# A two-layer sparse graph network on one Trainium2 core: a fourth buffer of queries, paid for with the room of the first products

## The chip, the cores and the metric

The kernel runs on one core of a Trainium2 chip (trn2). The metric is the device time of one execution in microseconds. Before the change the median of three runs was 2462.93 us (2452.32 to 2464.49). The profile comes from one more execution, of 2575.64 us, with the profiler on; its times are used for shares and for single operations, not as the metric.

## The reference

Eight graphs share one adjacency matrix of 2048 nodes (symmetric, with self loops, about one edge in 256), and each node has 256 features. All data are fp32.

- Layer 0 is attention with 4 heads of 64 features over the neighbours of a node. Scores are q.k / 8, clipped to [-10, 10]; where there is no edge, the score is -10. The softmax runs over each chunk of 256 keys by itself, and the results of the 8 chunks are added. Then come Wo, the bias, a residual, a layer norm with gamma and beta, once more + x, and a layer norm without weights.
- Layer 1 is graph attention: Wh = h W, logits leaky_relu(s_src[i] + s_dst[j]) on the edges, softmax over all neighbours, the weighted sum of Wh, elu, the residual and a layer norm.

```python
scores = clip(einsum('bhnd,bhjcd->bhnjc', q, kc) / 8, -10, 10); scores = where(mask == 0, -10, scores)
ctx = einsum('bhnjc,bhjcd->bhnd', softmax(scores, axis=-1), vc)
x = layernorm(x + (layernorm(ctx @ Wo.T + bo + x) * gamma + beta))
```

## The kernel before

The adjacency is so sparse that the kernel never forms a dense score matrix. It first builds, for each node, the list of its neighbours (`edge_lists`), sorts the nodes by their number of neighbours, and cuts them into 16 tiles of 128 nodes. A tile has as many slots as its busiest node has neighbours: `CAPS = (24, 14, 13, 12, 11, 11, 10, 10, 9, 9, 8, 8, 7, 7, 6, 5)`. (A node without an edge in a chunk is handled by constants, and a dense path for denser inputs is compiled in and not taken here.)

Batches are handled two at a time: there are 4 groups `g` of `G = 2` graphs, and 16 tiles `t` in each, so layer 0 has 64 steps. Layer 1 takes four graphs at a time: two passes of 16 tiles, of which the first is woven between the layer-0 steps of groups 2 and 3.

**Tables.** For each group, `tables(g, t)` turns 128 nodes of x into keys, values and queries on TensorE and writes them to DRAM: keys and values to `kv_d` (L369), queries to the first half of a row of `qx_d` (L380). Two tiles make a chunk of 256 nodes: `load_x` (L314) loads a chunk of x into an `xt` buffer, of which there are two, and `chunk_x` (L322) transposes it (L334) at even t. The second half of a `qx_d` row holds x + beta, which the end of layer 0 needs: at odd t GpSimd adds beta to the chunk in place (L352), and it is stored (L353). The tables of group 0 are made while the edge lists are built; those of group g + 1 during the steps of group g. Group 3's steps make none.

**Gathers.** `fetch0` (L504) gathers, for each slot of a tile, the keys and values of one neighbour per node, by an indirect DMA that GpSimd issues (L469). Two slots make a unit, and the units lie in a ring of `RING = 14` buffers, which layer 1 shares. A last one fetches the nodes' own queries and x + beta into a `qx` buffer (L507), of which there are three. A unit's buffer is free when its weighted values have been summed on TensorE (`summed`, L494). A `qx` buffer is free when `finish0` has made the layer norm with x + beta (L625), a step after the tile's scores.

**Scores.** `scores0` (L511) multiplies a unit's gathered keys by the queries on VectorE and sums the products over the features in one of two ways. For two thirds of the units (`npe = len(units) - len(units) // 3`, the first ones) VectorE writes the products (L530) and TensorE transposes and sums them in PSUM (L541, with ScalarE's copy L547 and the product with a selection matrix L551). For the last `len(units) // 3` units VectorE multiplies in place (L555) and sums with a reduction (L557). Products for TensorE go into room that is not used any more: those of unit i into the keys of unit i - 1. The first unit has none before it and uses a buffer of its own, `prod`. A tile with an odd number of slots has one slot in its last unit.

**Softmax, context, end.** `softmax0` clips the scores (L571) and normalizes them; `context0` weights the values on VectorE (L481) and ScalarE (L487) and sums them on TensorE (L494); `finish0` is Wo, the residual and the norms (L613 to L628), and `rows1` makes the table of layer 1. In step k the program writes, in this order: the gathers of step k + 1, the scores of step k, softmax and context of a layer-1 tile where there is one, `rows1` of i - 2, `finish0` of i - 1, the tables of the next group, softmax and context of step k.

That order is not the one on the engines. When the program is built, a planner of the framework orders each engine's instructions by the order of the program, but lets later ones go ahead where it reckons that an earlier one isn't ready. Each engine then follows its list strictly: in the trace a small VectorE operation of layer 1 (L665) stands at 212.21 us, before the first product of layer 0 at 263.00 us. So where an instruction stands in the program gives its rank, and the planner decides on its place.

Of the kernel before, what the change touches and what calls it, by code (L numbers as in the profile page):

```python
# [9 lines left out]
F32 = mybir.dt.float32  # L10
# [4 lines left out]
ALU = mybir.AluOpType  # L15
AX = mybir.AxisListType

P = 128
H = 4
D = 64  # L20
DP = 8
NJ = D // DP
# [14 lines left out]
G = 2  # L37
UNIT = 2
# [133 lines left out]
def sparse_path(ctx: ExitStack, tc: tile.TileContext, keep, x, adj, Wq, bq, Wk, bk, Wv, bv, Wo, bo, gamma, beta, W, a,  # L172
                out):
    nc = tc.nc
    B, N, F = x.shape
# [146 lines left out]
    def chunk_x(g, t):  # L322
# [18 lines left out]
        xTs[g, t] = xT, xC, xt  # L341
        return xT

    def tables(g, t):
        if t % 2 == 0:
            chunk_x(g, t)
        xT, xC, xt = xTs[g, t - t % 2]
        rows = slice(t % 2 * P, (t % 2 + 1) * P)
        if t % 2:

            xv = xt.rearrange("p k (b f) -> p (k b) f", b=G)
            nc.gpsimd.tensor_tensor(xv, xv, beta_r.unsqueeze(1).to_broadcast([P, 2 * G, F]), op=ALU.add)  # L352
            nc.sync.dma_start(qx_d[g][(t - 1) * P:(t + 1) * P, GF:].rearrange("(k p) f -> p k f", p=P), xt)  # L353
        kvs = work.tile([P, 2 * GF + 1], F32, tag="kvs", name="kvs", bufs=1)
        if g == PG:
            nc.scalar.copy(kvs[:, 2 * GF:], rank[:, t:t + 1])
        vk = kvs[:, 0:GF].rearrange("p (j b f) -> p b j f", b=G, j=NJ)
        for b in range(G):
            pm = bank("tk")
            for kc in range(KC):  # L360
                nc.tensor.matmul(pm[:, 0:F], xT[:, b * KC + kc, rows], wkv[:, kc, 0:F], start=(kc == 0), stop=False,  # L361
                                 skip_group_check=True)
            add_bias(pm[:, 0:F], biasT[:, 1])
            for kc in range(KC):
                nc.tensor.matmul(pm[:, F:], xC[:, b * KC + kc, rows], wkv[:, kc, F:], start=False, stop=(kc == KC - 1),  # L365
                                 skip_group_check=True)
            nc.scalar.copy(vk[:, b], pm[:, 0:F].rearrange("p (j f) -> p j f", j=NJ))
            nc.scalar.copy(kvs[:, GF + b * F:GF + (b + 1) * F], pm[:, F:])  # L368
        nc.sync.dma_start(kv_d[g][t * P:(t + 1) * P, :], kvs[:, 0:kv_d[g].shape[1]])  # L369
        q = bank("tk")  # L370
        for b in range(G):
            qb = q[:, b * F:(b + 1) * F]
            for kc in range(KC):
                nc.tensor.matmul(qb, xT[:, b * KC + kc, rows], wq[:, kc, :], start=(b == 0 and kc == 0), stop=False,  # L374
                                 skip_group_check=True)
            add_bias(qb, biasT[:, 0])
        qs = work.tile([P, GF], F32, tag="qs", name="qs", bufs=1)
        nc.scalar.copy(qs.rearrange("p (j b f) -> p b j f", b=G, j=NJ),
                       q.rearrange("p (b j f) -> p b j f", b=G, j=NJ))
        nc.sync.dma_start(qx_d[g][t * P:(t + 1) * P, 0:GF], qs)  # L380
        if t == NT - 1:

            tot = small.tile([P, G, KC], F32, tag="tot", name="tot", bufs=1)
            nc.vector.tensor_reduce(tot, xsum.pop(g), axis=AX.X, op=ALU.add)
            mv = small.tile([P, KC, G], F32, tag="mvs", name="mvs", bufs=1)
            pv = bank("tk")[:, 0:KC * G].rearrange("p (c b) -> p c b", c=KC)
            for oc in range(KC):
                for kc in range(KC):
                    nc.tensor.matmul(pv[:, oc, :], wkv[:, kc, F + oc * P:F + (oc + 1) * P], tot[:, :, kc],
                                     start=(oc == 0 and kc == 0), stop=(kc == KC - 1), skip_group_check=True)  # L390
            for oc in range(KC):
                nc.scalar.activation(mv[:, oc, :], pv[:, oc, :], AF.Identity, scale=-1.0, bias=bvc[:, oc:oc + 1])
            bO = small.tile([P, G, KC], F32, tag="bO", name="bO")
            po = bank("tk")[:, 0:KC * G].rearrange("p (c b) -> p c b", c=KC)
            for oc in range(KC):
                for kc in range(KC):
                    nc.tensor.matmul(po[:, oc, :], wo[:, kc, oc * P:(oc + 1) * P], mv[:, kc, :],
                                     start=(oc == 0 and kc == 0), stop=(kc == KC - 1), skip_group_check=True)
            for oc in range(KC):
                nc.scalar.activation(bO[:, :, oc], po[:, oc, :], AF.Identity, bias=biasT[:, 2, oc:oc + 1])  # L400
            biasO[g] = bO

    def first_tables(t):
        if t == 0:
            load_x(0, 0)
        if t % 2 == 0 and t + 2 < NT:
            load_x(0, t + 2)
        tables(0, t)

    with tc.tile_pool(name="lists", bufs=1) as pool:  # L410
# [92 lines left out]

    def fetch0(g, t):  # L504
        units = gather(kv_d[g].shape[1], kv_d[g], idx, t)
        qx = work.tile([P, 2 * GF], F32, tag="qx", name="qx", bufs=3)
        nc.gpsimd.indirect_dma_start(out=qx, out_offset=None, in_=qx_d[g],  # L507
                                     in_offset=bass.IndirectOffsetOnAxis(ap=node[:, t:t + 1], axis=0))
        got0[g, t] = qx, units

    def scores0(g, t):  # L511
# [2 lines left out]
        q = qx[:, 0:GF]  # L514
        sc = small.tile([P, GH, S], F32, tag="sc", name="sc")

        npe = len(units) - len(units) // 3
        ps_sc = bank("tf")[:, 0:GH * S].rearrange("p (s e) -> p s e", e=GH)
        W8 = GH * DP
        qv = q.rearrange("p (k j w) -> p k j w", k=UNIT, w=W8).unsqueeze(3)  # L520
# [1 line left out]
        def product(i):  # L522

            u, s0, n = units[i]
            if i:
                room = units[i - 1][0][:, :, 0:GF]
            else:
                room = work.tile([P, UNIT, GF], F32, tag="prod", name="prod", bufs=1)
            prod = room.rearrange("p k (j w) -> p k j w", w=UNIT * W8)[:, :, :, 0:n * W8]
            nc.vector.tensor_tensor(prod.rearrange("p k j (s w) -> p k j s w", w=W8),  # L530
                                    u[:, :, 0:GF].rearrange("p s (k j w) -> p k j s w", k=UNIT, w=W8),
                                    qv.to_broadcast([P, UNIT, NJ // UNIT, n, W8]), op=ALU.mult)
            return prod

        for i in range(0, npe, 4):
            some = units[i:min(i + 4, npe)]
            pr = bank("pr", 1).rearrange("p (k r) -> p k r", r=P)
            for k, (u, s0, n) in enumerate(some):
                prod = product(i + k)
                for j in range(NJ):  # L540
                    nc.tensor.matmul(pr[0:n * W8, k, :], prod[:, j // (NJ // UNIT), j % (NJ // UNIT), :], ident, is_transpose=True,  # L541
                                     start=(j == 0), stop=(j == NJ - 1), skip_group_check=True)
            m = len(some)
            prT = work.tile([P, 4, P], F32, tag="prT", name="prT", bufs=1)
            full = m - 1 if some[-1][2] < UNIT else m
            if full:
                nc.scalar.copy(prT[:, 0:full, :], pr[:, 0:full, :])  # L547
            if full < m:
                nc.scalar.copy(prT[0:W8, full, :], pr[0:W8, full, :])
            for k, (u, s0, n) in enumerate(some):  # L550
                nc.tensor.matmul(ps_sc[:, s0:s0 + n, :], prT[0:n * W8, k, :], sel[0:n * W8, 0:n * GH],  # L551
                                 start=(s0 == 0), stop=(k == m - 1 and i + m == npe), skip_group_check=True)
        for u, s0, n in units[npe:]:
            prod = u[:, :, 0:GF].rearrange("p s (j w) -> p s j w", w=W8)
            nc.vector.tensor_tensor(prod, prod, q.rearrange("p (j w) -> p j w", w=W8).unsqueeze(1)  # L555
                                    .to_broadcast([P, n, NJ, W8]), op=ALU.mult)
            nc.vector.tensor_reduce(sc[:, :, s0:s0 + n].rearrange("p e s -> p s e"),  # L557
                                    prod.rearrange("p s j (e d) -> p s e j d", d=DP),
                                    axis=AX.XY, op=ALU.add)
        st0[g, t] = ps_sc, sc, min(S, UNIT * npe)  # L560


# [3 lines left out]
    def softmax0(g, t):  # L566
        S = CAPS[t]
        n = GH * S
        ps_sc, sc, sp = st0.pop((g, t))
        for some, dots in ((sc[:, :, 0:sp], ps_sc[:, 0:sp, :].rearrange("p s e -> p e s")), (sc[:, :, sp:], sc[:, :, sp:])):  # L570
            nc.vector.tensor_scalar(some, dots, -10.0, 10.0, op0=ALU.max, op1=ALU.min)  # L571
        e = ebuf[:, 0:n]
        ev = e.rearrange("p (e s) -> p e s", s=S)
        nc.scalar.activation(ev, sc, AF.Exp)
# [198 lines left out]
            (fetch1 if layer else fetch0)(*at(i))  # L773
            fetched[0] += 1

    load_x(1, 0)
    fetch(0)
    waiting = None
    for k, (layer, i) in enumerate(seq):
# [6 lines left out]
        if layer == 0:  # L786
# [11 lines left out]
            if i:  # L798
                finish0(*at(i - 1))
            if g + 1 < NG:  # L800
                if i % 2 == 0 and i + NT + 2 < NG * NT:
                    load_x((i + NT + 2) // NT, (i + 2) % NT)
                tables(g + 1, i % NT)
            if tables_first:
                fetch(k + 1)
# [449 lines left out]
```

## Time and profile before

| | |
|---|---|
| median of 3 runs | 2462.93 us (2452.32 to 2464.49) |
| profiled execution | span 2573.9 us, 38911 instructions |
| TensorE matmul / weight load | 75% / 64% |
| VectorE | 71% |
| ScalarE | 55% |
| GpSimd | 58% |
| DMA | 669.10 MB; gathers and scatters of GpSimd 505.01 MB |
| granted TensorE clock | 0.864 |

A line of the groups reads: line of the kernel, engine, operation, what is written <- what is read, shapes, count | busy us, mean ns of one | idle time of the engine just before these instructions, and what ended most of it. A line of the waits reads: engine, tile and line that waited <- what ended the wait: us in total, times, the longest. A line of a timeline reads: start in us, us, engine, line, operation, shapes, count [idle time before <- what ended it]. PE is TensorE, DVE is VectorE, ACT is ScalarE, POOL is GpSimd and SP is SyncE; L507 is line 507 of the kernel. `acc`, `tk`, `tf`, `mf` and `pr` are banks of PSUM.

The stages as the trace shows them: up to some 209 us the edge lists and the tables of group 0; from 255.64 us, where the first unit is gathered, to about 2100 us layer 0, with layer 1 woven in from about 1225 us; after that layer 1 alone.

### The profile page before, as it was taken

What the parts mean: (1) busy time and instruction counts of PE and PEld (TensorE: products, weight loads), DVE (VectorE), ACT (ScalarE), POOL (GpSimd) and SP (SyncE); (2) the same over time, 40 slices, a digit from 0 to 9 for tenths busy, and PEclk for the clock granted to TensorE, in tenths of its full rate; (3) what the DMA queues carried; (4) which work ended last, traced back from release to release, by engine and by line L of the source; (5) the groups of instructions that cost most, each with busy time, mean ns of one, the idle gap of its engine ahead of it and who ended that gap; (6) DMA issues with size and microseconds to landing.
All of it is one profiled execution on the core that took longest, in us unless ns stands there. A gap on an engine that the chain in (4) does not pass through costs nothing. (4 is left out here: it accounts for less than half of the span.)

```text
span 2573.9 us, 38911 instructions
## 1 busy us (share of the span) xinstructions
PE 1940.6 (75%) x11946; PEld 1657.1 (64%) x11946; DVE 1833.1 (71%) x4071; ACT 1408.0 (55%) x5011; POOL 1505.4 (58%) x1225
## 2 busy tenths in 40 slices
PE   6787787688878879989888877775856786555764
PEld 5675676577666767777777765664756675444654
DVE  5865567767557777767878797776877877656765
ACT  3573353355545455555555665654454567556756
POOL 1123655475545655655677667566757753667764
PEclk9888897898899999899999988886977887777877
DMA  6744977497877868887769878867769874986763
GB/s 217 261 154 159 330 254 256 149 336 254 292 259 243 279 221 307 294 299 271 264 239 369 293 276 299 302 230 250 230 212 338 306 260 178 346 306 236 279 243 108
DMA packets 240749, 669.10 MB, mean 260 GB/s; under 512 B 44455, under 2 KB 70826, under 8 KB 238486
## 3 DMA queue, kind: packets, MB, share of 16 engines
q0 software_dynamic: 156800, 505.01, 56.8%
q1 hardware_dynamic: 80016, 151.56, 16.1%
q10 hardware_dynamic: 3718, 9.97, 1.2%
q8 instruction: 98, 1.61, 0.2%
q14 instruction: 117, 0.96, 0.1%
HBM read 612.79 MB, written 126.36 MB: 287 GB/s over the span
## 5 line engine op out<-in xcount | busy, mean ns | idle before, releaser
L469 POOL DMA_INDIRECT u<-kv_d,idx x656 | 829.1, 1264 | 348.7 <-PE acc L494 161.0
L494 PE MATMUL acc<-ident,u 128*128 128x128 f32 x5248 | 745.0, 299 | 200.0 <-DVE u L481 97.0
L494 PEld LDWEIGHTS acc<-ident,u 128*128 128x128 f32 x5248 | 666.8, 156 | 267.1 <-DVE u L481 137.9
L469 POOL DMA_INDIRECT u<-wh_d,idx x328 | 402.6, 1228 | 166.0 <-issue 77.4
L481 DVE TENSOR_TENSOR u<-u,al 128x1024 f32<-128x1024 f32 x280 | 337.2, 1238 | 1.2
L481 DVE TENSOR_TENSOR u<-u,z 128x1024 f32<-128x1024 f32 x266 | 314.8, 1214 | 0.8
L487 ACT ACTIVATE u<-u,z 128x64 f32<-128x64 f32 x1008 | 259.0, 336 | 24.9 <-DVE z L678 10.6
L541 PE MATMUL pr<-ident,u 128*128 128x128 f32 x1472 | 208.7, 291 | 55.7 <-DVE u L530 49.3
L530 DVE TENSOR_TENSOR u<-u,qx 128x1024 f32<-128x1024 f32 x184 | 228.7, 1243 | 26.4 <-DMA u<-kv_d,idx 20.8
L541 PEld LDWEIGHTS pr<-ident,u 128*128 128x128 f32 x1472 | 179.0, 150 | 76.1 <-DVE u L530 64.3
L487 ACT ACTIVATE u<-u,al 128x64 f32<-128x64 f32 x800 | 206.9, 341 | 34.6 <-DVE al L585 15.2
L641 PE MATMUL mf<-wa,x1T 128*128 128x264 f32 x512 | 172.4, 465 | 63.0 <-issue 19.9
L352 POOL TENSOR_TENSOR xt<-xt,beta_r 128x1024 f32<-128x1024 f32 x32 | 80.2, 2508 | 217.0 <-PE tk L334 178.1
L507 POOL DMA_INDIRECT qx<-qx_d,node x64 | 81.4, 1272 | 185.6 <-DVE o L625 114.8
L361 PE MATMUL tk<-wkv,xT 128*128 128x256 f32 x512 | 154.6, 418 | 21.3 <-ACT xC L339 14.9
L641 PEld LDWEIGHTS mf<-wa,x1T 128*128 128x128 f32 x512 | 102.2, 221 | 103.8 <-issue 41.2
L374 PE MATMUL tk<-wq,xT 128*128 128x256 f32 x512 | 146.8, 404 | 28.1 <-ACT kvs L368 20.9
L613 PE MATMUL mf<-wo,cT 128*128 128x256 f32 x512 | 145.5, 408 | 6.3 <-ACT whs L644 4.5
L365 PE MATMUL tk<-wkv,xC 128*128 128x256 f32 x512 | 147.4, 404 | 0.0
L435 ACT ACTIVATE sq<-o,nm 128x256 bf16<-128x256 f32 x256 | 129.5, 506 | 5.0
L619 DVE CUSTOM_DVE_ANT_0 o<-mf,qx 128x256 f32<-128x256 f32 x128 | 49.2, 420 | 104.7 <-PE mf L311 93.9
L712 PE MATMUL mf<-ident,hT 128*128 128x128 f32 x256 | 51.4, 333 | 95.6 <-DVE xr L716 42.8
(168 smaller groups left out, 3434.5 us busy)
## 6 DMA issues: line engine op xcount, KB each, us to landing
kv_d<-kvs SPq DMA_DIRECT2D x48, 512.0 KB
wh_d<-whs SPq DMA_DIRECT2D x64, 260.0 KB
xt<-in_x_dram SPq DMA_DIRECT2D x64, 256.0 KB
qx_d<-xt SPq DMA_DIRECT2D x32, 512.0 KB
qx_d<-qs SPq DMA_DIRECT2D x64, 256.0 KB
x_d<-o SPq DMA_DIRECT2D x64, 256.0 KB
xr<-x_d SPq DMA_DIRECT2D x32, 512.0 KB
u<-kv_d,idx POOLq DMA_INDIRECT x656
```

The costliest lines, as they stand in the source:

```text
L361: nc.tensor.matmul(pm[:, 0:F], xT[:, b * KC + kc, rows], wkv[:, kc, 0:F], start=(kc == 0), stop=False, skip_group_check=True)
L365: nc.tensor.matmul(pm[:, F:], xC[:, b * KC + kc, rows], wkv[:, kc, F:], start=False, stop=(kc == KC - 1), skip_group_check=True)
L374: nc.tensor.matmul(qb, xT[:, b * KC + kc, rows], wq[:, kc, :], start=(b == 0 and kc == 0), stop=False, skip_group_check=True)
L435: nc.scalar.activation(sq, src[:, k, :], AF.Square, bias=nm[:, k:k + 1], accum_out=m2[:, k:k + 1])
L469: nc.gpsimd.indirect_dma_start(out=u[:, k, 0:width], out_offset=None, in_=table, in_offset=bass.IndirectOffsetOnAxis(ap=idx[:, t, s0 + k:s ...
L481: nc.vector.tensor_tensor(pv, pv, av, op=ALU.mult)
L487: nc.scalar.activation(pe, pe, AF.Copy, scale=al[:, e, s0 + k:s0 + k + 1])
L494: nc.tensor.matmul(acc[:, c, :], part[:, k, c * P:(c + 1) * P], ident, is_transpose=True, start=first and k == 0 and c == 0, stop=last and ...
L530: nc.vector.tensor_tensor(prod.rearrange("p k j (s w) -> p k j s w", w=W8), u[:, :, 0:GF].rearrange("p s (k j w) -> p k j s w", k=UNIT, w=W8),
L541: nc.tensor.matmul(pr[0:n * W8, k, :], prod[:, j // (NJ // UNIT), j % (NJ // UNIT), :], ident, is_transpose=True, start=(j == 0), stop=(j ...
L613: nc.tensor.matmul(po[:, b, :], cT[:, b * KC + kc, :], wo[:, kc, :], start=(b == 0 and kc == 0), stop=False, skip_group_check=True)
L641: nc.tensor.matmul(pw[:, 0:F + 2 * H], xT[:, b * KC + kc, :], wa[:, kc, :], start=(kc == 0), stop=(kc == KC - 1))
```

## The change

Three parts, of which the second pays for the first in on-chip memory (`prod` and a `qx` buffer are both 4 KB per partition):

- `qx` gets four buffers in place of three.
- The first unit of a tile, and no longer the last one, is the one that VectorE always sums itself. Its keys are used up by that, so the products of the second unit can take their room, and `prod` goes. The number of units on each engine stays the same: `npe` is now one past the last TensorE unit, and units 1 to npe - 1 go to TensorE. The clipping of the scores is cut accordingly: slots 0 and 1 are clipped in place, like those of the last VectorE units.
- Beta is added to a chunk when the next chunk is begun (the last chunk of a group as before), so that GpSimd doesn't add right behind TensorE's transposes of the same chunk. The load of the chunk after next, which takes the buffer, moves into `tables` behind it, for all groups alike.

```diff
+    def add_beta(g, t):
+        xt = xTs.pop((g, t))[2]
+        xv = xt.rearrange("p k (b f) -> p (k b) f", b=G)
+        nc.gpsimd.tensor_tensor(xv, xv, beta_r.unsqueeze(1).to_broadcast([P, 2 * G, F]), op=ALU.add)
+        nc.sync.dma_start(qx_d[g][t * P:(t + 2) * P, GF:].rearrange("(k p) f -> p k f", p=P), xt)
+
     def tables(g, t):
         if t % 2 == 0:
+            if t:
+                add_beta(g, t - 2)
+            if g * NT + t + 2 < NG * NT:
+                load_x(*divmod(g * NT + t + 2, NT))
             chunk_x(g, t)
...
-        if t % 2:
-            xv = xt.rearrange("p k (b f) -> p (k b) f", b=G)
-            nc.gpsimd.tensor_tensor(xv, xv, beta_r.unsqueeze(1).to_broadcast([P, 2 * G, F]), op=ALU.add)
-            nc.sync.dma_start(qx_d[g][(t - 1) * P:(t + 1) * P, GF:].rearrange("(k p) f -> p k f", p=P), xt)
+        if t == NT - 1:
+            add_beta(g, t - 1)
...
-        qx = work.tile([P, 2 * GF], F32, tag="qx", name="qx", bufs=3)
+        qx = work.tile([P, 2 * GF], F32, tag="qx", name="qx", bufs=4)
...
-        npe = len(units) - len(units) // 3
+        npe = 1 + len(units) - len(units) // 3
...
-            if i:
-                room = units[i - 1][0][:, :, 0:GF]
-            else:
-                room = work.tile([P, UNIT, GF], F32, tag="prod", name="prod", bufs=1)
+            room = units[i - 1][0][:, :, 0:GF]
...
-        for i in range(0, npe, 4):
+        def reduced(u, s0, n):
+            prod = u[:, :, 0:GF].rearrange("p s (j w) -> p s j w", w=W8)
+            nc.vector.tensor_tensor(prod, prod, q.rearrange("p (j w) -> p j w", w=W8).unsqueeze(1)
+                                    .to_broadcast([P, n, NJ, W8]), op=ALU.mult)
+            nc.vector.tensor_reduce(sc[:, :, s0:s0 + n].rearrange("p e s -> p s e"),
+                                    prod.rearrange("p s j (e d) -> p s e j d", d=DP),
+                                    axis=AX.XY, op=ALU.add)
+        reduced(*units[0])
+        for i in range(1, npe, 4):
...
-                                 start=(s0 == 0), stop=(k == m - 1 and i + m == npe), skip_group_check=True)
-        for u, s0, n in units[npe:]:
...
+                                 start=(s0 == UNIT), stop=(k == m - 1 and i + m == npe), skip_group_check=True)
+        for unit in units[npe:]:
+            reduced(*unit)
...
-        for some, dots in ((sc[:, :, 0:sp], ps_sc[:, 0:sp, :].rearrange("p s e -> p e s")), (sc[:, :, sp:], sc[:, :, sp:])):
-            nc.vector.tensor_scalar(some, dots, -10.0, 10.0, op0=ALU.max, op1=ALU.min)
+        nc.vector.tensor_scalar(sc[:, :, UNIT:sp], ps_sc[:, UNIT:sp, :].rearrange("p s e -> p e s"), -10.0, 10.0, op0=ALU.max,
+                                op1=ALU.min)
+        for some in [sc[:, :, 0:UNIT]] + ([sc[:, :, sp:]] if sp < S else []):
+            nc.vector.tensor_scalar(some, some, -10.0, 10.0, op0=ALU.max, op1=ALU.min)
...
-    load_x(1, 0)
...
-                if i % 2 == 0 and i + NT + 2 < NG * NT:
-                    load_x((i + NT + 2) // NT, (i + 2) % NT)
```

More of the change, by code (lines that the diff above doesn't have):

```diff
@@ L405, in first_tables @@
             load_x(0, 0)
-        if t % 2 == 0 and t + 2 < NT:
-            load_x(0, t + 2)
         tables(0, t)
@@ L551, in scores0 @@
                 nc.tensor.matmul(ps_sc[:, s0:s0 + n, :], prT[0:n * W8, k, :], sel[0:n * W8, 0:n * GH],
-                                 start=(s0 == 0), stop=(k == m - 1 and i + m == npe), skip_group_check=True)
-        for u, s0, n in units[npe:]:
[L554 to L559, printed above, removed]
+                                 start=(s0 == UNIT), stop=(k == m - 1 and i + m == npe), skip_group_check=True)
+        for unit in units[npe:]:
+            reduced(*unit)
         st0[g, t] = ps_sc, sc, min(S, UNIT * npe)
```

## The prediction

> **What bounds the kernel now.** I read the page's first two parts, then the groups with shapes kept apart, the waits, and the timelines of GpSimd and VectorE.
>
> ```profile
> PE 1940.6 (75%) x11946; PEld 1657.1 (64%) x11946; DVE 1833.1 (71%) x4071; ACT 1408.0 (55%) x5011; POOL 1505.4 (58%) x1225
> DMA  6744977497877868887769878867769874986763
> ```
>
> No engine is full and none is far from it, so the time is handed back and forth between queues. What counts is who makes TensorE and VectorE wait. The change touches only layer 0 (the first query gather stands at 209 us, the last layer-0 product ends near 2100 us), so the last 470 us can only shift.
>
> The groups give the prices:
>
> ```profile
> L507 POOL DMA_INDIRECT qx<-qx_d,node x64 | 81.4, 1272 | 185.6 <-DVE o L625 114.8 <-DVE ebuf L575 18.2 <-DVE sc L571 15.2
> L352 POOL TENSOR_TENSOR xt<-xt,beta_r 128x1024 f32<-128x1024 f32 x32 | 80.2, 2508 | 217.0 <-PE tk L334 178.1 <-issue 22.8 <-DMA beta_r<-in_L_gnn_beta_dram 15.8
> L530 DVE TENSOR_TENSOR prod<-u,qx 128x1024 f32<-128x1024 f32 x64 | 79.2, 1238 | 52.8 <-DMA qx<-qx_d,node 26.1 <-DMA u<-kv_d,idx 25.4 <-issue 1.3
> L555 DVE TENSOR_TENSOR u<-u,qx 128x1024 f32<-128x1024 f32 x64 | 77.9, 1218 | 6.2 <-DMA u<-kv_d,idx 5.2 <-PE tf L305 0.8 <-PE acc L494 0.2
> L557 DVE TENSOR_REDUCE sc<-u 128x16 f32<-128x1024 f32 x64 | 77.4, 1212 | 0.2
> L557 DVE TENSOR_REDUCE sc<-u 128x8 f32<-128x512 f32 x32 | 21.8, 680 | 0.1
> ```
>
> The waits say who is hurt:
>
> ```profile
> POOL u L469 <- PE acc L494: 223.1, 89, 19.0
> POOL xt L352 <- PE tk L334: 178.1, 11, 22.5
> POOL qx L507 <- DVE o L625: 114.8, 20, 19.1
> PE pr L541 <- DVE u L530: 49.3, 39, 4.6
> PE pr L541 <- DVE prod L530: 39.2, 12, 13.0
> DVE prod L530 <- DMA qx<-qx_d,node: 26.1, 10, 9.7
> DVE prod L530 <- DMA u<-kv_d,idx: 25.4, 5, 10.7
> DVE u L530 <- DMA u<-kv_d,idx: 20.8, 10, 5.3
> ```
>
> GpSimd waits 114.8 us for finish0 to give a query buffer back, and 26.1 + 25.4 + 20.8 us of VectorE's idle time end with a query or a unit landing. The timeline of GpSimd shows what stands behind:
>
> ```profile
> 476.47 4.64 POOL L352 TENSOR_TENSOR xt<-xt,beta_r 128x1024 f32<-128x1024 f32 x2
> ...
> 587.73 0.99 POOL L469 DMA_INDIRECT u<-kv_d,idx  x1 [0.30 <-issue]
> 607.84 1.70 POOL L507 DMA_INDIRECT qx<-qx_d,node  x1 [19.11 <-DVE o L625]
> 609.84 0.99 POOL L469 DMA_INDIRECT u<-kv_d,idx  x1 [0.30 <-issue]
> ```
>
> For 19.11 us the queue stands on one query gather, and the unit gather after it goes at once, with no wait of its own. VectorE's timeline shows the order in which a tile's scores are made:
>
> ```profile
> 472.12 1.23 DVE L530 TENSOR_TENSOR prod<-u,qx 128x1024 f32<-128x1024 f32 x1 [9.74 <-DMA qx<-qx_d,node]
> 473.26 1.22 DVE L555 TENSOR_TENSOR u<-u,qx 128x1024 f32<-128x1024 f32 x1
> 474.40 1.22 DVE L530 TENSOR_TENSOR u<-u,qx 128x1024 f32<-128x1024 f32 x1
> 475.54 1.21 DVE L557 TENSOR_REDUCE sc<-u 128x16 f32<-128x1024 f32 x1
> 476.67 5.54 DVE L530 TENSOR_TENSOR u<-u,qx 128x1024 f32<-128x1024 f32 x1
> ```
>
> The units that VectorE sums itself already stand between the products for TensorE, although the program writes them last. The 5.54 us one overlaps the two beta additions above.
>
> **The skill.** Perfetto Trace Analysis, section Tensor Engine Instruction, says that ACT, DVE and GPSIMD are strict FIFOs; the 19.11 us stall agrees. The same page, Optimization Strategy, takes a repeating gap as a sign of too few buffers; 20 stalls on one buffer's release agree. VectorE: DVE Perf Modes, perf-mode tier table, has fp32 tensor_tensor at 1x (2293 ns for 2048 elements) and tensor_reduce at 1x; half of that for 1024 agrees with 1218 and 1212 ns here. Perfetto Trace Analysis, Optimizing Scalar/DVE Operations, says that GPSIMD and DVE share an SBUF port; 5.54 us in place of 1.22 beside two additions agrees.
>
> **Part by part.** *Fourth query buffer.* With three, the query of step k+1 needs finish0 of k-2, done in step k-1; with four, finish0 of k-3, a whole step (20 to 30 us here) earlier. The 26.1 us in which VectorE waits for a query should go. Of the 114.8 us on GpSimd only that part helps which unit gathers can use: the ring of 14 units already stops them for 223.1 us. VectorE waits for units 25.4 + 20.8 + 5.2 (L555) = 51.4 us; the first landing (10.7 us) has nothing to do with queries and ring and transfer time stay. I credit half, 26 us. The bounds are 0 and the whole GpSimd wait, 114.8 us.
>
> *First unit on VectorE.* The number of units on each engine stays: before, VectorE takes len//3 last ones; after, the first and len//3 - 1 last ones. In the tiles of 9, 9, 7, 7 and 5 slots the one VectorE unit was the half-filled last one and is now a full one: 5 tiles x 4 groups = 20 sums at 1.21 in place of 0.68 us, +10.6 us of VectorE. The multiplications are the same, only divided otherwise. ScalarE gets 20 more short copies of a half unit, and at 55% busy hides them. The first product comes after a multiplication and a sum, 1.22 + 1.21 = 2.4 us later, and TensorE's transposes wait behind it. But in the timeline above the fourth instruction already was the sum: four multiplications and a sum take VectorE equally long in either order, the last product of a four-unit tile comes at the same time, and TensorE has tables, rows1 and finish0 to do. I take 0, with a bound of 2.4 us in each of 64 steps. Clamping: a tile with more than one VectorE unit (6 tiles, 24 steps) gets a third tensor_scalar, at 0.17 us (L571) 4.1 us.
>
> *Beta a chunk later.* The same 32 additions of 2.5 us. Most of their 178.1 us of waiting lies before 255 us, where no unit gather stands behind them. Later, the ring stops the gathers anyway after most of them. Stores of x + beta and the loads behind them on SyncE move a step; a wait of the load for that store exists today (52.0 us in 21 times, 5.2 at most). Behind it are the stores of keys, values and queries, for whose buffers ScalarE waits. The load is wanted two steps later. I take 0, and say plus or minus 10.
>
> *Sum.* 26.1 + 26 - 10.6 - 4.1 = 37 us of the profiled 2575.64. The timed median is 0.956 of that run, so 36 us: 2462.93 - 36 = 2427 us.
>
> **Rivals.** *The ring takes over.* Unit gathers start no earlier; only the 26.1 us go: 26.1 - 14.7 = 11 us, 2452 us, within 0.5%. For it: 223.1 us on the ring. Against it: the gather at 609.84 went without a wait of its own.
>
> *Slower: TensorE starts late.* If in half of the steps one sum is laid bare, 32 x 1.21 = 39 us; with only the query waits saved, 39 + 14.7 - 26.1 = 27 us, 2489 us. For it: TensorE waits 49.3 + 39.2 us for products, and the last group has no tables to fill in. All 64 steps at 1.21 would give 2526 us. Against it: the interleaving above.
>
> *All of GpSimd's wait comes through.* 114.8 - 14.7 = 100, times 0.956: 2367 us. For it: VectorE, TensorE and ScalarE all wait for gathers now and then. Against it: VectorE waits for landings in layer 0 for under 80 us in all.
>
> **Chances.** The forecast 0.43, everything through 0.12, the ring 0.17, slower 0.28. That gives faster 0.55, same 0.17, slower 0.28. The range runs from 2385 (between forecast and 2367) to 2508 (between 2489 and 2526) and leaves out about 1 in 10 on each side.
>
> **What would show it.** Right: L507 loses most of its 114.8 us behind L625, VectorE's wait for queries is below 8 us, L557 has 84 full and 12 half sums, and TensorE's wait for L530's successor stays near 90 us. Wrong: waits for products well above 130 us (the slower rival), the wait of L469 for L494 growing by what L507 loses (the ring), or stores on SyncE that keep ScalarE waiting longer for kvs than today's 35.0 + 24.5 us.

## The result and the profile after

| | before | after |
|---|---|---|
| median of 4 runs each | 2463.71 us (2452.32 to 2473.20) | 2429.31 us (2424.80 to 2440.35) |
| ratio | | 0.9865 [0.982, 0.991] |
| profiled execution | 2573.9 us, clock 0.864 | 2423.1 us, clock 0.892 |

The change makes the kernel 34 us faster. The two profiled executions can't be compared as they stand: their granted TensorE clocks are 0.864 and 0.892, and that of before took 2573.9 us, 110 us more than the median of before. So the kernel before was profiled once more (run e8_before_again, span 2458.0 us at clock 0.889), and the change too (e5_after_again, 2446.2 us at 0.889). Readings of before against after below are taken from these two, on one chip; the two executions differ by 12 us, the medians of that chip by 29, so they show where time moves better than how much. The ratios leave out executions that lie over 1.5% above the fastest of their kernel and the medians don't (of e2, 7 of 14 are left out), so sizes of parts are given below as the ratio's distance from 1, times the median of before.

The page of after, its first two parts:

```profile
PE 1885.1 (78%) x11946; PEld 1618.3 (67%) x11946; DVE 1842.2 (76%) x4095; ACT 1401.9 (58%) x5031; POOL 1472.6 (61%) x1225
...
DMA  6745877598879679598879979896679975986873
```

VectorE runs 24 instructions and 9 us more than before (1833.1), on 4095 instructions. The groups of after with shapes kept apart give the prices and the counts:

```profile
L540 DVE TENSOR_TENSOR u<-u,qx 128x1024 f32<-128x1024 f32 x84 | 102.3, 1219 | 42.4 <-DMA qx<-qx_d,node 23.9 <-DMA u<-kv_d,idx 18.5
L542 DVE TENSOR_REDUCE sc<-u 128x16 f32<-128x1024 f32 x84 | 101.9, 1214 | 0.6
L513 POOL DMA_INDIRECT qx<-qx_d,node x64 | 75.1, 1173 | 73.9 <-DVE o L633 27.3 <-issue 11.6 <-DVE sc L576 8.6
L540 DVE TENSOR_TENSOR u<-u,qx 128x512 f32<-128x512 f32 x12 | 8.1, 679 | 2.2 <-DMA u<-kv_d,idx 2.2
L542 DVE TENSOR_REDUCE sc<-u 128x8 f32<-128x512 f32 x12 | 8.1, 677 | 0.0
```

L540 and L542 are the multiplication and the sum of a unit that VectorE sums itself: 84 full and 12 half ones. L513, the gather of the queries, waits 27.3 us for finish0 (L633) in place of 114.8. No engine is full (78% at most).

The waits of before at the higher clock, to compare with:

```profile
POOL u L469 <- PE acc L494: 174.1, 111, 14.1
POOL qx L507 <- DVE o L625: 94.8, 17, 11.7
DVE o L619 <- PE mf L311: 79.9, 35, 7.4
DVE sc L571 <- PE tf L551: 67.5, 42, 5.0
PE pr L541 <- DVE u L530: 54.9, 42, 4.6
PE pr L541 <- DVE prod L530: 47.7, 17, 13.1
DVE prod L530 <- DMA qx<-qx_d,node: 27.6, 10, 9.8
DVE u L530 <- DMA u<-kv_d,idx: 26.9, 12, 5.9
DVE prod L530 <- DMA u<-kv_d,idx: 26.1, 5, 13.1
```

and those of the change on the same chip:

```profile
POOL u L475 <- PE acc L500: 238.6, 113, 17.8
DVE sc L576 <- PE tf L562: 123.4, 44, 8.7
PE pr L552 <- DVE u L533: 66.0, 43, 6.2
DVE o L627 <- PE mf L311: 56.3, 30, 5.9
DVE u L533 <- DMA u<-kv_d,idx: 28.6, 14, 5.2
POOL qx L513 <- DVE o L633: 25.1, 7, 5.6
DVE u L540 <- DMA qx<-qx_d,node: 24.2, 10, 4.4
DVE u L540 <- DMA u<-kv_d,idx: 19.0, 4, 16.4
```

Four readings. GpSimd's wait for a query buffer falls by 69.7 us, and its wait for a free unit of the ring rises by 64.5: most of the stall has only changed its name. VectorE's wait for queries stays (27.6, then 24.2), now on the first unit's multiplication. A new cost stands where VectorE clips the scores (L571, now L576): it waits 123.4 us for TensorE in place of 67.5. And two waits shrink: TensorE's for products (54.9 + 47.7 to 66.0) and VectorE's for the result of Wo in finish0 (L619, now L627: 79.9 to 56.3).

The windows by stage, cut where the last context product (L494, in the change L500) of steps 8, 31 and 66 ends, steps of layer 1 counted too. Before at the higher clock; columns are length, busy us and count of PE, PEld, DVE, ACT and POOL, granted clock, DMA share, GB/s:

```profile
508.00:1069.00 561.00, 482.04 (x3068) 411.99 (x3067) 412.67 (x838) 299.35 (x1161) 340.93 (x270) 0.94 0.83 289
1069.00:1845.00 776.00, 632.47 (x4229) 547.49 (x4228) 636.99 (x1323) 469.44 (x1724) 543.96 (x418) 0.91 0.82 289
1845.00:2458.00 613.00, 387.51 (x2554) 332.90 (x2553) 443.98 (x1080) 390.59 (x1377) 412.73 (x337) 0.81 0.76 272
```

and the change on the same chip:

```profile
510.00:1043.00 533.00, 475.83 (x3049) 408.15 (x3048) 412.04 (x842) 296.27 (x1154) 310.97 (x250) 0.95 0.81 285
1043.00:1834.00 791.00, 646.93 (x4297) 561.11 (x4295) 646.25 (x1337) 474.92 (x1760) 552.27 (x436) 0.92 0.84 297
1834.00:2446.00 612.00, 385.21 (x2560) 332.22 (x2558) 442.65 (x1079) 388.33 (x1379) 411.76 (x336) 0.82 0.76 271
```

The stage in which layer 0 is alone is 28 us shorter; the one in which layer 1 is woven in is 15 us longer; the rest is the same. The woven stage of the change also holds 68 more TensorE instructions (4297 against 4229) with 14 us of busy time, so part of its 15 us is work that now stands there.

### The profile page after: what moved, and what is told of

Its sections match the earlier page's. It is cut to its first block, busy times and chain, and to the rows that moved or that the text cites. A ratio compares the mean times of both kernels' runs of the same rounds, so it can differ in the third digit from the quotient of the medians.

```text
span 2423.1 us, 38937 instructions
## 1 busy us (share of the span) xinstructions
PE 1885.1 (78%) x11946; PEld 1618.3 (67%) x11946; DVE 1842.2 (76%) x4095; ACT 1401.9 (58%) x5031; POOL 1472.6 (61%) x1225
## 5 line engine op out<-in xcount | busy, mean ns | idle before, releaser
L475 POOL DMA_INDIRECT u<-kv_d,idx x656 | 802.2, 1223 | 423.0 <-PE acc L500 159.2
L500 PE MATMUL acc<-ident,u 128*128 128x128 f32 x5248 | 727.7, 295 | 191.6 <-DVE u L487 118.4
L500 PEld LDWEIGHTS acc<-ident,u 128*128 128x128 f32 x5248 | 649.9, 153 | 254.8 <-DVE u L487 166.1
L552 PE MATMUL pr<-ident,u 128*128 128x128 f32 (+1 forms) x1984 | 280.5, 291 | 78.5 <-DVE u L533 62.4
L533 DVE TENSOR_TENSOR u<-u,qx 128x1024 f32<-128x1024 f32 (+1 forms) x248 | 296.4, 1195 | 32.1 <-DMA u<-kv_d,idx 25.7
L552 PEld LDWEIGHTS pr<-ident,u 128*128 128x128 f32 (+1 forms) x1984 | 240.9, 148 | 108.0 <-DVE u L533 85.7
L649 PE MATMUL mf<-wa,x1T 128*128 128x264 f32 x512 | 158.5, 435 | 21.0 <-ACT x1T L644 10.9
L369 PE MATMUL tk<-wkv,xT 128*128 128x256 f32 x512 | 144.9, 396 | 14.7 <-ACT xC L339 14.5
L621 PE MATMUL mf<-wo,cT 128*128 128x256 f32 x512 | 144.8, 406 | 10.6 <-ACT whs L652 9.9
L540 DVE TENSOR_TENSOR u<-u,qx 128x1024 f32<-128x1024 f32 (+1 forms) x96 | 110.3, 1152 | 44.6 <-DMA qx<-qx_d,node 23.9
L382 PEld LDWEIGHTS tk<-wq,xT 128*128 128x128 f32 x512 | 94.4, 204 | 51.0 <-ACT kvs L376 42.0
L437 ACT ACTIVATE nm<-sums 128x2 f32<-128x2 f32 (+1 forms) x160 | 32.4, 202 | 160.0 <-DVE sums L627 82.0
```

The source lines that it names most:

```text
L475: nc.gpsimd.indirect_dma_start(out=u[:, k, 0:width], out_offset=None, in_=table, in_offset=bass.IndirectOffsetOnAxis(ap=idx[:, t, s0 + k:s ...
L500: nc.tensor.matmul(acc[:, c, :], part[:, k, c * P:(c + 1) * P], ident, is_transpose=True, start=first and k == 0 and c == 0, stop=last and ...
L621: nc.tensor.matmul(po[:, b, :], cT[:, b * KC + kc, :], wo[:, kc, :], start=(b == 0 and kc == 0), stop=False, skip_group_check=True)
L649: nc.tensor.matmul(pw[:, 0:F + 2 * H], xT[:, b * KC + kc, :], wa[:, kc, :], start=(kc == 0), stop=(kc == KC - 1))
```

## The experiments

The kernels ran in three groups. Each group ran on one chip with the kernel before beside it, and a ratio is always to that. The chips are not alike: before took a median of 2615.47 us on the first, 2468.39 us on the second and 2569.1 us on the third, and the profiles show a granted clock of 0.861 to 0.871 on the first and the third and of 0.884 to 0.889 on the second.

My theory was that of the prediction: the fourth buffer gives some 50 us, the longer sums take back some 15, and the sum ahead of the first product and the later beta cost nothing. The rival was that the sum ahead of the first product costs tens of microseconds, so that the buffer gains more than the whole shows.

One thing goes with every edit and is parted from it by no run: the planner lays out the instructions of all engines anew. e1 and e2 have the same 4095 instructions of VectorE in different orders, though their programs differ in one number. Two builds of one program have the same order on every chip (e1 and e9, e2 and e10, after, e5 and e11). So a difference between two kernels is that of the edit and of the order that came with it.

### Parts added one after the other (first chip)

**e1_unit_only**: before, with the part that frees the room and nothing else.

```diff
-        npe = len(units) - len(units) // 3
+        npe = 1 + len(units) - len(units) // 3
...
+            room = units[i - 1][0][:, :, 0:GF]
...
+        reduced(*units[0])
+        for i in range(1, npe, 4):
```

> The first unit on VectorE and no prod buffer, but three query buffers and beta at its old place. If the fourth buffer makes the gain, this costs the 10.6 us of longer sums and 4 us of clamps and saves nothing: 2464 + 14 = 2478 us, a ratio of 1.000 to 1.010. If the new order of the units makes it (sums that fill VectorE's idle time, no wait for the prod buffer): 0.987. If late beta makes it: 1.006 as well.

Measured: 2696.94 us, ratio 1.0316 [1.0259, 1.0373], 83 us slower.

**e2_qx4**: e1 with the fourth query buffer.

```diff
-        qx = work.tile([P, 2 * GF], F32, tag="qx", name="qx", bufs=3)
+        qx = work.tile([P, 2 * GF], F32, tag="qx", name="qx", bufs=4)
```

> The first unit on VectorE and four query buffers, beta at its old place. If the fourth buffer makes the gain: the whole of it, a ratio of 0.983 to 0.990, about 2429 us. If late beta makes it: 1.000 to 1.006, since only the cost is left. If the order of the units makes it: 0.987.

Measured: 2637.45 us, ratio 1.0027 [0.9983, 1.0071]. The fourth buffer gives back 76 of the 83 us (59 by the medians).

**e3_unit_beta**: the change with three query buffers, which is e1 with the later beta.

```diff
-        qx = work.tile([P, 2 * GF], F32, tag="qx", name="qx", bufs=4)
+        qx = work.tile([P, 2 * GF], F32, tag="qx", name="qx", bufs=3)
```

> The change without the fourth buffer: first unit on VectorE, beta a chunk later, three query buffers. If the fourth buffer makes the gain: 1.000 to 1.010. If the order of the units or late beta makes it: 0.987. GpSimd's wait at the query gather for finish0 should be back to about 115 us in every case.

Measured: 2642.88 us, ratio 1.0101 [1.0045, 1.0157].

**e4_beta_only**: before, with beta a chunk later and nothing else.

```diff
+            if t:
+                add_beta(g, t - 2)
+            if g * NT + t + 2 < NG * NT:
+                load_x(*divmod(g * NT + t + 2, NT))
             chunk_x(g, t)
...
+        if t == NT - 1:
+            add_beta(g, t - 1)
```

> The kernel before with beta a chunk later alone. If late beta does nothing: 0.996 to 1.004, and the additions stand at nearly the same places of GpSimd's list, with three of them still ahead of the first unit gather. If it makes the gain: 0.990 or less, and GpSimd's wait for TensorE's transposes falls from 178 us to under 90.

Measured: 2645.50 us, ratio 1.0118 [1.0085, 1.0152].

GpSimd's waits in e1:

```profile
POOL u L469 <- PE acc L494: 340.7, 99, 32.1
POOL qx L507 <- DVE o L627: 138.9, 17, 17.5
```

and in e2:

```profile
POOL u L469 <- PE acc L494: 360.4, 94, 17.4
```

VectorE waits for TensorE at two places above all. In the profiles of the first and the third chip a part of these waits carries another releaser's name, or none ("remote", "issue"), so I take all idle time before the line. The clipping and finish0, in the first profile of before (at a like clock):

```profile
L571 DVE TENSOR_SCALAR sc<-tf 128x64 f32<-128x64 f32 (+3 forms) x64 | 14.1, 220 | 90.5 <-PE tf L551 51.5 <-PE tk L365 12.8 <-issue 10.0
L619 DVE CUSTOM_DVE_ANT_0 o<-mf,qx 128x256 f32<-128x256 f32 x128 | 49.2, 420 | 104.7 <-PE mf L311 93.9 <-PE acc L494 5.1 <-issue 4.0
```

in e1:

```profile
L570 DVE TENSOR_SCALAR sc<-tf 128x64 f32<-128x64 f32 (+5 forms) x64 | 14.0, 218 | 182.2 <-PE tf L556 141.5 <-remote 21.8 <-PE tf L305 11.9
L621 DVE CUSTOM_DVE_ANT_0 o<-mf,qx 128x256 f32<-128x256 f32 x128 | 49.2, 420 | 146.5 <-PE mf L311 139.5 <-issue 5.0 <-remote 1.7
```

and in e2:

```profile
L570 DVE TENSOR_SCALAR sc<-tf 128x64 f32<-128x64 f32 (+5 forms) x64 | 13.9, 218 | 171.6 <-PE tf L556 120.8 <-remote 14.9 <-issue 11.4
L621 DVE CUSTOM_DVE_ANT_0 o<-mf,qx 128x256 f32<-128x256 f32 x128 | 49.4, 421 | 139.4 <-PE mf L311 92.8 <-remote 27.6 <-issue 18.5
```

Moving the first unit brings the idle time at the clipping from 90.5 to 182.2 us. It isn't TensorE's wait for products that grew (57.8 us in e1, 49.3 + 39.2 in before), which is where I had said that the cost would show. I read it so: TensorE gets a tile's first products later, does other work meanwhile, and VectorE pays at the other end, when it wants the scores. The fourth buffer takes little from that wait, and little from that in finish0 (146.5 to 139.4 us).

Each of the two kernels also has one long stall. In e1, amid the steps of group 2, VectorE stands once for 30.82 us before a small sum for the tables of group 3 (L384), which the planner has put ahead of the next tile's scores and which waits for ScalarE's copies of the transposed x:

```profile
1380.57 0.19 DVE L384 TENSOR_REDUCE tot<-xs 128x4 f32<-128x32 f32 x1 [30.82 <-ACT xT L336]
```

In e2 this wait is 0.6 us. There, as group 2 begins, GpSimd stands 37.39 us before a unit gather, for the tables of that group to land, and VectorE after it 27.57 us in finish0:

```profile
1095.14 1.00 POOL L469 DMA_INDIRECT u<-kv_d,idx  x1 [37.39 <-DMA kv_d<-kvs]
1126.56 0.42 DVE L621 CUSTOM_DVE_ANT_0 o<-mf,qx 128x256 f32<-128x256 f32 x1 [27.57 <-remote]
```

No profile of before or of the change has either stall, though the change has the same first unit and the same fourth buffer. So up to 31 of e1's 83 us come from where one instruction was put.

Beta alone costs 1.2%, yet e3 is 56 us faster than e1 (1.0316 to 1.0101). Up to 31 us of that is the stall at L384, which e3 doesn't have. The part has no sign of its own.

### The same unit, without the sum ahead (second chip)

**e5_after_again** is the change once more.

> The whole change once more, beside the runs of before of this call. If the gain belongs to the change on any chip: a ratio of 0.980 to 0.992. If it hangs on how fast TensorE is allowed to run, it is near 1.00 wherever before takes some 2615 us, as it did for the four runs above.

Measured: 2439.04 us, ratio 0.988 [0.9851, 0.9908].

**e6_first_late**: before, with the first unit summed on VectorE as in the change, but written after the products, with `prod` kept for the second unit.

```diff
+        npe = 1 + len(units) - len(units) // 3
...
-            if i:
+            if i > 1:
...
-        for i in range(0, npe, 4):
+        for i in range(1, npe, 4):
...
-        for u, s0, n in units[npe:]:
+        for u, s0, n in units[0:1] + units[npe:]:
```

> The kernel before, with the first unit on VectorE in place of the last, but summed after the products, which keep the prod buffer: the same 20 longer sums and 24 clamps as the change, and no sum ahead of the first product. If the sum ahead of TensorE's first product is what costs in the first of the four runs: 1.000 to 1.010. If the unit chosen, with its longer sums, costs: 1.02 to 1.035, as there.

Measured: 2490.46 us, ratio 1.0086 [1.0061, 1.0112]: 21 us (15 to 28), where the longer sums and the clips had been put at 14.7. The wait at the clipping is 86.1 us, against 67.5 in before and 123.4 in the change.

Whether the first product comes later can be read off VectorE's timeline. The table is worked out from all 64 tiles of each run (a product is here one that TensorE sums). It has, counted from where the clipping of the tile before starts, the means without the first tile and the two at the stalls, in us:

| | first product ends | last product ends | clipping starts |
|---|---|---|---|
| before, first profile (clock 0.864) | 14.7 | 23.2 | 29.0 |
| e1 and e9: unit | 16.7 and 16.7 | 23.1 and 23.1 | 29.9 and 29.6 |
| e2 and e10: unit, fourth buffer | 13.6 and 13.3 | 21.1 and 20.6 | 29.0 and 28.3 |
| before, e8 (clock 0.889) | 13.8 | 22.1 | 27.4 |
| e6: first unit summed late | 13.8 | 22.0 | 27.4 |
| the change, e5 | 12.4 | 20.0 | 27.1 |

With the unit summed first, the first product for TensorE ends 2.0 us later, the last one at the same time, and the clipping starts 0.6 to 0.9 us later, some 34 to 53 us over 61 tiles. Summed last, none of the three moves by 0.1 us. So of the 44 to 52 us that the unit costs beside the stall, some 23 to 31 go with the late first product, and 21 with VectorE doing more. The first product waits for the program's order, and for the room, which is the keys that the sum of the first unit reads; no run parts the two, nor either from the planner's new order. The fourth buffer shows here too: the last product ends 2.0 and 2.5 us earlier, and the clipping starts 0.9 and 1.3 us earlier. The step from 21 us to e1's 83 is across two chips, and so a size and not an exact difference.

**e7_gather_first**: the change, with GpSimd's additions of beta for group 1 queued behind the unit gathers of the second tile.

```diff
+        with tc.issue_after(gathers[0]) if g == 1 else nullcontext():
+            nc.gpsimd.tensor_tensor(xv, xv, beta_r.unsqueeze(1).to_broadcast([P, 2 * G, F]), op=ALU.add)
...
+        if len(fetches) < 2:
+            fetches.append(1)
+            gathers[:] = [ins.ins]
```

Here `ins` is the unit gather issued last, so that `gathers[0]` ends up as the last one of the second tile.

> The whole change, and group 1's beta additions queued on GpSimd behind the second tile's gathers. If the three additions ahead of the first unit gather hold it up: the first unit is gathered near 217 us in place of 252, VectorE's first wait of 15 us goes, and the time falls by 10 to 20 us against the change (0.4 to 0.8%). If the memsets of the ring on VectorE set that start, or TensorE's tables only move into the steps: no change within 0.3%.

Why this: GpSimd's timeline of after shows three additions in the queue ahead of the first unit gather. Two of them wait for the transposes of their chunks (16.52 and 17.93 us), and the gathers stand behind them.

```profile
210.32 2.35 POOL L348 TENSOR_TENSOR xt<-xt,beta_r 128x1024 f32<-128x1024 f32 x1 [2.26 <-issue]
229.19 2.36 POOL L348 TENSOR_TENSOR xt<-xt,beta_r 128x1024 f32<-128x1024 f32 x1 [16.52 <-PE tk L334]
249.47 2.35 POOL L348 TENSOR_TENSOR xt<-xt,beta_r 128x1024 f32<-128x1024 f32 x1 [17.93 <-PE tk L334]
251.97 1.02 POOL L475 DMA_INDIRECT u<-kv_d,idx  x1
```

The first multiplication then waits 15.22 us for that gather, on VectorE's timeline of after:

```profile
258.94 1.23 DVE L540 TENSOR_TENSOR u<-u,qx 128x1024 f32<-128x1024 f32 x1 [15.22 <-DMA u<-kv_d,idx]
```

Measured for e7: 2406.58 us, ratio 0.9747 [0.9724, 0.9771], 32 us under e5 on the same chip. This version beats both kernels. Its first gather on GpSimd:

```profile
219.01 1.01 POOL L479 DMA_INDIRECT u<-kv_d,idx  x1 [4.27 <-ACT xT L337]
```

and VectorE at the first multiplication:

```profile
244.63 1.79 DVE L432 MEMSET u<- 128x2080 f32 x1 [0.38 <-issue]
246.34 1.16 DVE L547 TENSOR_TENSOR u<-u,qx 128x1024 f32<-128x1024 f32 x1
```

The gathers go 33 us earlier, and the multiplication follows VectorE's clearing of the ring without a wait, 12.6 us earlier than in after. The change of beta had the aim of keeping additions out of GpSimd's way; ahead of the first gathers, the planner had left three of them there. But the early start is not shown to be what gains the 32 us. The last context product of step 0 ends 30 us earlier than in e5 (264 against 294 us), that of step 8 17 us earlier (493 against 510) and that of step 16 only 2 us (673 against 675); from there to step 31 the lead grows to 24 us again (1019 against 1043). The order of all engines changed with this edit too, and what gains time after step 16 is open.

**e8_before_again** is the kernel before, for a profile at this clock.

> The kernel before once more, for a profile from the chip of these runs: a ratio of 0.995 to 1.005.

Measured: 2459.71 us; its waits and stages are shown above.

### The parts once more, and the change beside them (third chip)

**e9_unit_only_again** and **e10_qx4_again** are e1 and e2, **e11_after_third** is the change.

> The first unit on VectorE alone, once more. The longer sums and clamps cost 0.9% (the run that sums it after the products). If the sum ahead of the first product costs besides, as a wait of VectorE for TensorE's scores: 1.015 to 1.03, with that wait above 100 us. If the 3% of the first time belonged to that chip's slower TensorE: 1.005 to 1.012.

> The first unit on VectorE and four query buffers, beta at its old place, once more. If the fourth buffer carries the gain and late beta nothing: the ratio of the whole change within 0.3%. If late beta carries part of it: above the whole change by 0.5% or more.

> The whole change beside the two runs above on one chip: 0.988 where before takes about 2465 us; where it takes about 2615 us, 0.985 to 1.00.

| run | us | ratio |
|---|---|---|
| e9: unit | 2647.10 | 1.0293 [1.0238, 1.0347] |
| e10: unit, fourth buffer | 2583.00 | 1.0036 [1.0008, 1.0064] |
| e11: unit, fourth buffer, beta (the change) | 2605.08 | 1.0148 [1.0088, 1.0208] |

e9 and e10 repeat e1 and e2: 75 us lost, 66 won back (78 and 64 by the medians). They have the same order as e1 and e2, and the same stalls, 30.82 us at L384 and 27.37 us at L621. VectorE's idle time for e9:

```profile
L570 DVE TENSOR_SCALAR sc<-tf 128x64 f32<-128x64 f32 (+5 forms) x64 | 14.0, 218 | 157.9 <-PE tf L556 106.3 <-PE tf L305 18.7 <-remote 17.1
L621 DVE CUSTOM_DVE_ANT_0 o<-mf,qx 128x256 f32<-128x256 f32 x128 | 49.2, 420 | 150.4 <-PE mf L311 117.3 <-PE pr L546 12.7 <-PE tk L311 7.7
```

and for e10:

```profile
L570 DVE TENSOR_SCALAR sc<-tf 128x64 f32<-128x64 f32 (+5 forms) x64 | 13.9, 218 | 167.7 <-PE tf L556 121.8 <-PE mf L643 14.8 <-PE tk L311 13.2
L621 DVE CUSTOM_DVE_ANT_0 o<-mf,qx 128x256 f32<-128x256 f32 x128 | 49.4, 420 | 123.2 <-PE mf L311 68.2 <-remote 32.2 <-issue 14.4
```

The buffer takes nothing from the idle time at the clipping here (157.9 and 167.7 us), and 27 us from that in finish0 (150.4 and 123.2).

But the whole change is 1.5% slower on this chip, and 1.2% faster on the second. The stages of e11:

```profile
526.00:1086.00 560.00, 479.16 (x3047) 409.18 (x3045) 409.54 (x842) 296.44 (x1146) 309.49 (x251) 0.94 0.77 271
1086.00:1963.00 877.00, 668.53 (x4294) 573.25 (x4293) 645.22 (x1337) 476.95 (x1763) 541.67 (x436) 0.88 0.77 268
1963.00:2607.00 644.00, 396.45 (x2558) 343.39 (x2556) 442.62 (x1079) 389.99 (x1379) 407.06 (x337) 0.78 0.73 258
```

In the first profile of before (clock 0.864; whether it is from the same chip isn't on record) the same stages, cut by the same rule, took 585, 826 and 642 us. So the gain where layer 0 is alone is there at both clocks (28 us at the higher, 25 at the lower), and the loss in the woven stage is 15 us at the higher clock and 51 at the lower. That stage has the granted clock 0.92 in e5 and 0.88 in e11. That TensorE, being slower, makes each late start dearer would fit, but it is only argued: no run changes the clock and nothing else. The order alone is no cause here: e5 and e11 have the same one, and so have the two profiles of before. With beta later, the fourth buffer isn't measured on one chip: e3 has 1.0101 on the first, e11 1.0148 on the third, which doesn't look like a gain.

**e12_before_gather_first**: before, with the additions of group 1 queued behind the second tile's gathers, as in e7.

```diff
-            nc.gpsimd.tensor_tensor(xv, xv, beta_r.unsqueeze(1).to_broadcast([P, 2 * G, F]), op=ALU.add)
+            with tc.issue_after(gathers[0]) if g == 1 else nullcontext():
+                nc.gpsimd.tensor_tensor(xv, xv, beta_r.unsqueeze(1).to_broadcast([P, 2 * G, F]), op=ALU.add)
```

> The kernel before with group 1's beta additions behind the second tile's gathers and nothing else. If the start of the gathers is worth the same in both kernels: 0.982 to 0.992, with the first unit gathered near 225 us in place of 255. If the gain over the change needed the fourth buffer (more gathers that can use the time): 0.995 or more.

Measured: 2569.56 us, ratio 1.0017 [0.9993, 1.0041]. Step 0's last context product ends at 258 us, where it ended at 287 us in the first profile of before; by step 31 the lead has shrunk from 29 to 19 us (1087 against 1106), and at step 66 e12 is 17 us behind (1949 against 1932). An early start is no gain if the middle takes it back. Whether it would hold for before at the higher clock wasn't tried.

Four query buffers with `prod` kept, which would have measured the buffer by itself, weren't tried; whether there is room for both isn't on record.

## Why the prediction came out right, and where its steps were wrong

The total, 2427 us against 2429.31, is right, and the direction. But terms of the sum were wrong against each other, and the runs say so; that they cancel to 2 us is luck.

- **Right.** The 114.8 us of L507 behind finish0 went (27.3 left; at like clock 94.8 to 25.1). The counts, 84 full and 12 half sums, are as worked out. The fourth buffer was put at 52 us; with the unit's part in place it measured 76 and 66 us (e1 to e2, e9 to e10; 59 and 64 by the medians), the orders and one stall of some 30 us on each side included. The Trainium skill (Perfetto Trace Analysis, Optimization Strategy) says that a gap that keeps repeating can mean too few buffers; the 66 to 76 us agree with it. ScalarE's wait for kvs, named as a sign of stores in the way, didn't grow (49.1 + 28.0 to 58.4 + 18.0 us).
- **Failed: "I take 0" for the first product behind the sum.** This was the step that was most wrong. With the sums (10.6 + 4.1 = 14.7 us) the unit's part was put at 14.7 us; it measured 83 and 75 us on the chips at the lower clock. 21 us (15 to 28) of such a cost are the sums and clips (e6, at the higher clock), and up to 31 us are the stall at L384, which another order doesn't have. Some 20 to 30 us remain for the late first product, 0.4 us a step, between 0 and the bound of 2.4 us x 64 = 154 us. That the last product comes at the same time in either order was right (23.2 and 23.1 us after the clipping before) and beside the point: the first product ends 2.0 us later and the clipping starts 0.6 to 0.9 us later; at like clock VectorE's idle time there is 67.5 us in before and 123.4 in the change. The sign that I had named, TensorE's wait for products, fell from 102.6 to 66.0 us.
- **Half right: the gain.** The 26.1 us of VectorE's query waits did not go (27.6 to 24.2 at the higher clock), and its waits for units fell only from 26.9 + 26.1 + 7.7 (L555) = 60.7 to 28.6 + 19.0 = 47.6 us. No single wait has the gain. What shows is that VectorE's products come earlier after the clipping before: the last one ends 2.0 to 2.5 us earlier with the buffer at the lower clock, and 2.1 us earlier in the change at the higher. Queries that come earlier would do that, and so would the order: with the fourth buffer the planner has put 29 of the 64 query gathers further forward in GpSimd's list, on the mean of all by some 6 or 7 gathers, and none further back. No run parts the two.
- **The ring.** I gave its sign as the wait of L469 for L494 growing by what L507 loses. Read off the first profile it didn't grow (223.1 to 225.8), but at like clock it did: 64.5 us against 69.7. So the rival's mechanism is there. Its time, 2452 us, isn't: all four runs of after lie below it (2424.80 to 2440.35).
- **Beta, 0 plus or minus 10 us.** Too narrow: +31 us alone (e4), -56 us with the unit (e1 to e3), of which up to 31 are the stall at L384, and +29 us with unit and buffer (e10 to e11). The argument that no unit gather stands behind the additions before 255 us was wrong for the last two of them, which wait 14.16 and 15.23 us for transposes with the first unit gather next in the queue:

```profile
253.15 2.35 POOL L352 TENSOR_TENSOR xt<-xt,beta_r 128x1024 f32<-128x1024 f32 x1 [15.23 <-PE tk L334]
255.64 1.02 POOL L469 DMA_INDIRECT u<-kv_d,idx  x1
```

- **The factor 0.956.** I took 2575.64 against 2462.93 us for the cost of profiling. It was an execution at a lower granted clock (0.864): the profiled execution of after is one of its timed runs, at 2424.8 us and 0.892.
- **What remains.** At the lower clock the parts sum to no gain, and the whole change is slower. e1, e2 and e4 were not run at the higher clock, so which part is cheaper there, and gives the change its 1.2 to 1.4%, is open. The order that the planner makes anew with every edit has no term in the prediction. Its share isn't measured by itself, but the single stalls of 27 to 31 us show that it can be as large as a part.

The slower rival, 2489 us, had the right mechanism for the unit and the right order of size for the bared sums, 39 us against some 20 to 30. What it lacked was the buffer's gain, which is larger.

## What to carry to other kernels

A part that frees memory for another part has a price of its own: ask who gets its first operand later, and look for the cost where the result is wanted, too, not only where the operand is: here it stood at VectorE's clipping, while TensorE's wait for operands fell. When a stall on a strict queue is removed, look for the next wait in the same queue before counting the gain, and compare profiles of like clock only. Take all idle time before a line, not one releaser's row. And where a planner orders the engines' lists, look for single long stalls before reading the difference between two kernels as the price of an edit: one misplaced instruction was up to 31 of 83 us here. An early start need not last: e7's lead of 30 us at step 0 was 2 us at step 16, and e12's was lost by step 66.

## What was not expected of the hardware

- The same kernel took a median of 2468.39, 2569.1 and 2615.47 us on three chips, with granted TensorE clocks of 0.877 to 0.890, 0.859 to 0.877 and 0.854 to 0.869 in these executions: 6% between the fastest and the slowest, several times the effect of the change. The mean clocks (0.882 and 0.861) differ by 2.4%, so the time isn't in proportion to them; why is open.
- The sign of a change can hang on the chip: 0.988 [0.985, 0.991] on one and 1.015 [1.009, 1.021] on another, for one and the same kernel, with the same order on every engine.
